# Two samples in one count matmul, evicted as 16-bit pairs, and dense layers over three tiles

## The chip, the core and the metric

The kernel runs on one NeuronCore of a Trainium2 chip. Five engines work side by side, each with its own queue in program order: TensorE (PE for its matmuls, PEld for its weight loads), VectorE (DVE), ScalarE (ACT), GpSimd (POOL) and SyncE (SP). The metric is the device time of one execution in microseconds (us): for the kernel before, the median of three runs is 7548.09 us (7520.87 to 7551.03).

## The reference

A recommender's forward pass over a batch of 16384 samples. Each sample has 32 word indices, three lists of 20 indices into small tables and four single indices:

```python
tok = word_emb[token_idx].mean(axis=1)          # 50000 x 300 table, 32 rows a sample
e1 = emb_mh1[mh1_idx].mean(axis=1)              # 1000 x 64;  e2: 5000 x 64;  e3: 10000 x 64
o1 = emb_oh1[oh1_idx]                           # 100 x 64;   o2: 50;  o3: 20;  o4: 1000
emb = jnp.concatenate([tok, e1, e2, e3, o1, o2, o3, o4], axis=1)      # 748 columns
wide = wide_mh1[mh1_idx].sum(axis=(1, 2)) + ...                       # one number a table row
h = relu(emb @ W1 + b1); h = relu(h @ W2 + b2); h = relu(h @ W3 + b3) # 1024, 512, 256
return sigmoid(h @ Wd + bd + wide)
```

## The kernel before, in words

The batch is cut into 128 tiles of 128 samples. Four streams of work run over the tiles at once.

**Words.** `tokens` issues one indirect DMA on POOL for each of the 32 word columns of a tile (line 255; 4096 in all, 128 rows of 300 floats each). Two of them fill one buffer of the pool `tok` and make a group; DVE adds a group's two halves to a running sum (lines 237, 239, 243; 16 groups a tile). The sum lags the issue by `TOK_LAG` = 3 groups in program order, and the pool has `TOK_BUFS` = 8 buffers, so a gather can be issued once the group 8 before it has been added.

**Counts.** The small tables are not gathered. Their rows are cut into 138 slices of 128 rows (`n_h`). For each sample DVE writes a one-hot of the row within the slice and a one-hot of the slice for its 64 lookups (`one_hots`, line 322). The lookups of two samples lie on the two halves of the 128 partitions. `counts` multiplies the two one-hots on TensorE, once for each half (K = 64, line 340), which gives the 128 x 138 matrix of counts of a sample; ACT evicts twelve such matrices in one instruction as fp8 (line 347). A tile has 11 steps (`STEPS`) of six pairs of samples, the last of four. There is one buffer of four PSUM banks for it (`ps_c`).

**Small sums.** `small_sums` (line 365) multiplies the counts of a whole tile (the weights: 128 samples of one slice, which lie 138 bytes apart) by the table in three bf16 terms (195 columns), 138 matmuls a tile.

**Layers.** Blocks of two tiles (`LAYER_TILES`, 256 columns, fp32) go through the three layers and the output row (lines 461, 470, 486), paced so that a block ends when the next one is ready. The last two tiles are blocks of one. A matmul in fp32 stands in the trace as two records.

The main loop is written out by hand: in each of 1424 steps it issues, in this order, the next step's one-hots, this step's count matmuls and eviction, transposes that are due, a share of the word gathers and sums, an eleventh or so of a tile's small-table matmuls and a share of the layers. Every engine keeps that order.

Of the kernel before, what the change touches and what calls it, by code (L numbers as in the profile page):

```python
# [8 lines left out]
F32 = mybir.dt.float32  # L9
# [3 lines left out]
U32 = mybir.dt.uint32  # L13
AF = mybir.ActivationFunctionType
# [10 lines left out]
TOK_BUFS = 8  # L25
# [3 lines left out]
LAYER_TILES = 2  # L29
HALF = P // 2  # L30
N_SMALL = 3 * N_MH + 4
# [20 lines left out]
def kernel(  # L52
# [42 lines left out]
    wp = ctx.enter_context(tc.tile_pool(name="wide", bufs=4))  # L95
    xsp = ctx.enter_context(tc.tile_pool(name="x_small", bufs=3))
# [3 lines left out]
    ps_c = ctx.enter_context(tc.tile_pool(name="ps_c", bufs=1, space=bass.MemoryType.PSUM))  # L100
# [47 lines left out]
    minus_half = const.tile([P, P], BF16, name="minus_half")  # L148
    nc.vector.tensor_single_scalar(minus_half, ident, -0.5, op=ALU.mult)
# [17 lines left out]
    def convert_tables():  # L167
# [19 lines left out]
        def make(p, c):  # L187

            if c == 0:
                nc.scalar.activation(term(p, 0), rows(p), AF.Copy, scale=2.0)  # L190
                return
            _, a, b = pieces[p]
            left = ps_h.tile([P, SPLIT, ROW], F32, name="left", tag="ph")[:, 0 : b - a, :]
            nc.tensor.matmul(left, ident, rows(p), start=True, stop=False)  # L194
            for k in range(c):
                nc.tensor.matmul(left, minus_half, term(p, k), start=False, stop=(k == c - 1))
            nc.scalar.activation(term(p, c), left, AF.Copy, scale=2.0)

# [67 lines left out]
    def load_indices(blk):  # L266
# [8 lines left out]
        for s in range(NSUB):  # L275
            nc.sync.dma_start(
                out=ix[(s % 2) * HALF : (s % 2 + 1) * HALF, s // 2],
                in_=idx[b0 + s * P : b0 + (s + 1) * P, IDX_MH:IDX_COLS].rearrange(
                    "(f p) c -> p f c", p=HALF
                ),  # L280
            )
# [32 lines left out]
    def one_hots(sc, s, i):  # L314
# [5 lines left out]
        for w, (one, n) in enumerate(((row1, P), (slice1, n_h))):  # L320
# [6 lines left out]
            )  # L327
        return row1, slice1

    def counts(cnt, hot, i):  # L330
# [4 lines left out]
        pc = ps_c.tile([P, 2, 2, 512], F32, name="pc")  # L335
        for k in range(rows):
            for f in range(2):
                half = slice(f * HALF, (f + 1) * HALF)
                at = k % n * n_h
                nc.tensor.matmul(  # L340
                    pc[:, f, k // n, at : at + n_h],
                    hot[0][half, k, :],
                    hot[1][half, k, :],
                    start=True,
                    stop=True,
                )
        nc.scalar.activation(  # L347
            cnt[:, :, b : b + rows, :].rearrange("l f (g k) h -> l f g (k h)", g=2),
            pc[:, :, :, 0 : n * n_h],
            AF.Copy,  # L350
            scale=0.5,
            saturate=False,
        )

    def small_sums(g, cnt):


        by_slice = cnt.rearrange("l f p h -> l (f p) h")
        for i in (0, 2, 4, 6):
            pair = SMALL[i : i + 2]  # L360
            pg = ps_g.tile([P, 2, 3 * ROW], F32, name="pg")
            for j, f in enumerate(pair):
                h0, h1 = slices[f]
                for h in range(h0, h1):
                    nc.tensor.matmul(  # L365
                        pg[:, j, :], by_slice[:, :, h], terms[:, h, :], start=(h == h0), stop=(h == h1 - 1)
# [70 lines left out]
    def early_part(block):  # L437


        part = ps_c.tile([P, 4, 512], F32, name="pc")  # L440
        for m in range(4):
            for k in range(NK - 3):
                nc.tensor.matmul(
                    part[:, m, 0 : block.n],
                    w1_sb[: chunk_k[k], k, m * P : (m + 1) * P],
                    block.chunk(k),
                    start=(k == 0),
                    stop=False,
                )
        return part  # L450

    def layer(dst, weights, bias, srcs, n_out, part=None):

        n = srcs[0].shape[-1]
        for m in range(n_out):
            begun = part is not None and m < 4
            ph = part[:, m, :] if begun else ps_h.tile([P, N], F32, name="ph", tag="ph")
# [84 lines left out]
    sizes = [LAYER_TILES] * (tiles // LAYER_TILES - 1) + [1] * LAYER_TILES  # L542
# [27 lines left out]
    for step in range(n_steps):  # L570
        t, i = divmod(step, STEPS)
        s = t % NSUB
        if i == 0:
# [7 lines left out]
            if t < tiles:  # L581
                if s == 0 and t:
                    sc = next_sc
                cnt = cp.tile([P, 2, HALF, n_h], FP8, name="cnt", tag="counts")
# [79 lines left out]
```

## Time and profile before

| | |
|---|---|
| median of three runs | 7548.09 us (7520.87 to 7551.03) |
| profiled execution: span from first to last instruction | 5191.3 us |
| busy in the span: PE, PEld | 5113.7 us (99%), 4177.5 us (80%) |
| busy in the span: DVE, ACT, POOL | 3890.9 us (75%), 2600.7 us (50%), 3888.4 us (75%) |
| mean granted TensorE clock | 0.998 |
| gathers: busy, and idle of POOL before them | 3887.5 us, 1260.5 us |

The page gives no time for the profiled execution other than its span. The median of the runs is 2356.8 us longer, and no view shows what lies in that difference. A busy PE includes matmuls that wait in its pipeline for one another, so its 99% is not a rate; the rates are read from rows of the timeline, where a burst of equal matmuls stands with its start and its count.

### The profile page before, as it was taken

Reading aid. Unit: us, or ns where it says so; the run is one execution under the profiler, and the core shown is the slowest. Engines: PE = TensorE matmul, PEld = TensorE weight load, DVE = VectorE, ACT = ScalarE, POOL = GpSimd, SP = SyncE. Lnnn points to the kernel's source line nnn. Section 1 sums busy time; section 2 is a strip of 40 time slices with the busy share of each in tenths; the row PEclk is TensorE's granted clock in tenths of the full one; section 3 lists DMA queues with packets and bytes.
Section 4 is the critical chain, followed back from the end, with each engine's and each line's share of the span. In section 5 each row is a group of like instructions: output and inputs, shape, how many; then the busy total and the mean of one; then the engine's idle time right before and its main releaser. Section 6 shows DMA issues by size and latency. Waiting matters only on the chain.

```text
span 5191.3 us, 116518 instructions
## 1 busy us (share of the span) xinstructions
PE 5113.7 (99%) x46912; PEld 4177.5 (80%) x46912; DVE 3890.9 (75%) x8502; ACT 2600.7 (50%) x2445; POOL 3888.4 (75%) x4103
## 2 busy tenths in 40 slices
PE   7999999999999999999999999999999999999999
PEld 5888888888888888888888888888888878888888
DVE  6777777777777777777777777777777777777773
ACT  6555555555545545545445455555555545555552
POOL 7777777777777777777777777777777777777774
PEclk9999999999999999999999999999999999999999
DMA  7444444444444444444444444444444444444442
GB/s 201 123 126 125 125 126 124 125 126 125 126 124 126 125 126 125 126 124 126 125 126 126 124 126 125 126 126 123 125 125 126 125 126 124 126 125 126 124 124 77
DMA packets 253019, 653.38 MB, mean 126 GB/s; under 512 B 119056, under 2 KB 119633, under 8 KB 252477
## 3 DMA queue, kind: packets, MB, share of 16 engines
q0 software_dynamic: 196608, 629.41, 44.2%
q1 hardware_dynamic: 55869, 16.53, 1.4%
q8 instruction: 367, 6.01, 0.5%
q14 instruction: 175, 1.43, 0.1%
HBM read 645.59 MB, written 0.07 MB: 124 GB/s over the span
## 4 chain that ended last, share of the span: by engine, by line
PE 94%; DVE 2%; issue 1%; DMA 1%; ACT 0%; POOL 0%; SPq 0%; DVEq 0%; ACTq 0%
PE ph L461 46%; PE pg L365 32%; PE pc L340 12%; PE po L486 1%; PE pt L426 1%; PE pt L410 1%; PE pt L407 1%; DMA tok_rows<-in_word_emb_dram,it 1%; DVE own L239 1%; DVE own L243 0%; DMA w_sb<-in_W_dram 0%; POOL tok_rows L255 0%; DVE slice L322 0%; PE left L194 0%; PE pt L427 0%
## 5 line engine op out<-in xcount | busy, mean ns | idle before, releaser
L255 POOL DMA_INDIRECT tok_rows<-in_word_emb_dram,it x4096 | 3887.5, 949 | 1260.5 <-issue 873.6
L347 ACT ACTIVATE cnt<-pc 128x1656 fp8e3<-128x1656 f32 (+1 forms) x1408 | 2124.6, 1509 | 1607.7 <-PE pc L340 1592.1
L365 PE MATMUL pg<-terms,cnt 128*128 128x195 bf16 x17664 | 1828.7, 253 | 7.9 <-DVE g L371 7.6
L365 PEld LDWEIGHTS <-cnt 128*128 128x128 fp8e3 x17664 | 1590.3, 144 | 162.1 <-issue 31.8
L461 PE MATMUL ph<-h,w_sb 128*128 128x256 f32 (+1 forms) x5200 | 1224.2, 379 | 0.5 <-ACT h L470 0.5
L461 PE MATMUL ph<-x_small,w_sb 128*128 128x256 f32 (+2 forms) x4128 | 1044.4, 381 | 4.8 <-DVE x_small L429 3.0
L461 PEld LDWEIGHTS ph<-h,w_sb 128*128 128x128 f32 x5200 | 930.8, 191 | 99.2 <-issue 0.8
L322 DVE TENSOR_TENSOR row<-own,sc 128x768 bf16<-128x768 bf16 (+1 forms) x1408 | 762.3, 541 | 304.2 <-PE pc L340 251.5
L239 DVE TENSOR_TENSOR own<-own,tok_rows 128x300 f32<-128x300 f32 x1920 | 917.0, 478 | 63.3
L243 DVE TENSOR_TENSOR own<-own,tok_rows 128x300 f32<-128x300 f32 x1792 | 856.8, 478 | 61.8
L340 PEld LDWEIGHTS <-row 64*128 64x128 bf16 x16384 | 495.4, 94 | 484.8 <-issue 227.5
L470 ACT ACTIVATE h<-ph,b_sb 128x256 f32<-128x256 f32 (+1 forms) x906 | 426.8, 471 | 912.3 <-PE ph L461 912.0
L461 PEld LDWEIGHTS ph<-x_small,w_sb 128*128 128x128 f32 (+1 forms) x4128 | 739.3, 191 | 86.6 <-PE ph L461 6.4
L322 DVE TENSOR_TENSOR slice<-own,sc 128x828 bf16<-128x828 bf16 (+1 forms) x1408 | 795.5, 565 | 0.0
L340 PE MATMUL pc<-slice,row 64*128 64x138 bf16 x16384 | 751.0, 223 | 15.8 <-DVE slice L322 9.0
L461 PE MATMUL ph<-x_tok,w_sb 128*128 128x256 f32 (+1 forms) x2064 | 565.4, 380 | 0.0
L371 DVE TENSOR_REDUCE g<-pg 128x130 f32<-128x390 f32 (+1 forms) x512 | 261.1, 510 | 393.6 <-PE pg L365 391.0
L461 PEld LDWEIGHTS ph<-x_tok,w_sb 128*128 128x128 f32 x2064 | 373.0, 192 | 40.9
L428 DVE TENSOR_SCALAR x_tok<-pt 128x256 f32<-128x256 f32 x128 | 54.4, 425 | 301.6 <-PE pt L427 301.6
L411 DVE TENSOR_TENSOR x_small<-pt,scale 128x384 f32<-128x384 f32 x128 | 71.2, 556 | 91.8 <-PE pt L410 91.8
L486 PE MATMUL po<-h,wd_sb 128*1 128x256 f32 (+1 forms) x260 | 68.0, 374 | 1.6 <-DVE x_small L429 1.0
L490 DVE TENSOR_TENSOR h<-po,wide_row 1x256 f32<-1x256 f32 (+1 forms) x65 | 26.5, 408 | 54.9 <-PE po L486 51.9
(55 smaller groups left out, 872.4 us busy)
## 6 DMA issues: line engine op xcount, KB each, us to landing
tok_rows<-in_word_emb_dram,it POOLq DMA_INDIRECT x4096
ix<-in_idx_dram SPq DMA_DIRECT2D x128, 32.0 KB
w_sb<-in_W_dram SPq DMA_DIRECT2D x6, 512.0 KB
raw<-in_mh_dram SPq DMA_DIRECT2D x4, 682.5 KB
it<-in_idx_dram SPq DMA_DIRECT2D x32, 64.0 KB
w_sb<-in_W_dram SPq DMA_DIRECT2D x1, 2048.0 KB
out_dram<-h SPq DMA_DIRECT2D x63, 1.0 KB
raw<-in_mh_dram SPq DMA_DIRECT2D x2, 227.5 KB
```

The lines of the kernel that those rows point to most:

```text
L239: nc.vector.tensor_add(tok_sum, tok_sum, a)
L243: nc.vector.tensor_add(to, tok_sum, b)
L255: nc.gpsimd.indirect_dma_start(out=rows[:, r * TOK_D : (r + 1) * TOK_D], out_offset=None, in_=word, in_offset=bass.IndirectOffsetOnAxis(ap ...
L322: nc.vector.tensor_tensor(one[:, 0:rows, :].rearrange("p i (n d) -> p i n d", d=2), iota[:, 0:n].rearrange("p (n d) -> p n d", d=2).unsque ...
L340: nc.tensor.matmul(pc[:, f, k // n, at : at + n_h], hot[0][half, k, :], hot[1][half, k, :], start=True, stop=True,)
L347: nc.scalar.activation(cnt[:, :, b : b + rows, :].rearrange("l f (g k) h -> l f g (k h)", g=2), pc[:, :, :, 0 : n * n_h], AF.Copy, scale=0 ...
L365: nc.tensor.matmul(pg[:, j, :], by_slice[:, :, h], terms[:, h, :], start=(h == h0), stop=(h == h1 - 1))
L371: nc.vector.tensor_reduce(g[:, at : at + n * ROW].rearrange("p (f d) -> p f d", f=n), pg[:, 0:n, :].rearrange("p f (c d) -> p f d c", c=3) ...
L411: nc.vector.tensor_tensor(self.small[:, 0:3, at], pt[:, 0:3, :], scale.unsqueeze(2).to_broadcast([P, 3, P]), ALU.mult)
L461: nc.tensor.matmul(ph[:, 0:n], weights[: src.shape[0], k, m * P : (m + 1) * P], src, start=(k == 0), stop=(k == len(srcs) - 1),)
L470: nc.scalar.activation(dst[:, m, 0:n], ph[:, 0:n], AF.Relu, bias=bias[:, m : m + 1])
L486: nc.tensor.matmul(po[:, 0:n], wd_sb[:, k : k + 1], h3[:, k, 0:n], start=(k == 0), stop=(k == M3 - 1))
```

## The change

The two samples of a pair now share one matmul. Their one-hots still lie on the two halves of the partitions, but the row one-hot of the upper half is multiplied by 256 (a new ACT instruction in place, on 64 partitions), and one matmul with K = 128 gives count(lower) + 256 x count(upper). ACT evicts six such matrices as 16-bit integers, whose two bytes are the two counts. Read as fp8, a byte k is the number k/64, so the table's terms are scaled by 64 where they were scaled by 2. The counts lie as slice, pair, byte: the 128 samples of one slice are contiguous. The samples of a pair are now neighbours in the batch (the index load is rearranged to match). The counts' PSUM tile halves to two banks and has two buffers.

The layers run over blocks of three tiles (384 columns), still with two blocks of one tile at the end. Six word buffers instead of eight, two buffers of small features instead of three, two of the wide rows instead of four.

```diff
-TOK_BUFS = 8
+TOK_BUFS = 6
-LAYER_TILES = 2
+LAYER_TILES = 3
+LAST_TILES = 2
+UPPER = 256.0
+COUNT = 64.0
...
-    wp = ctx.enter_context(tc.tile_pool(name="wide", bufs=4))
-    xsp = ctx.enter_context(tc.tile_pool(name="x_small", bufs=3))
+    wp = ctx.enter_context(tc.tile_pool(name="wide", bufs=2))
+    xsp = ctx.enter_context(tc.tile_pool(name="x_small", bufs=2))
...
-    ps_c = ctx.enter_context(tc.tile_pool(name="ps_c", bufs=1, space=bass.MemoryType.PSUM))
+    ps_c = ctx.enter_context(tc.tile_pool(name="ps_c", bufs=2, space=bass.MemoryType.PSUM))
...
-                nc.scalar.activation(term(p, 0), rows(p), AF.Copy, scale=2.0)
+                nc.scalar.activation(term(p, 0), rows(p), AF.Copy, scale=COUNT)
...
+        upper = row1[HALF:P, 0:rows, :]
+        nc.scalar.activation(upper, upper, AF.Copy, scale=UPPER)
         return row1, slice1
...
-        pc = ps_c.tile([P, 2, 2, 512], F32, name="pc")
+        pc = ps_c.tile([P, 2, 512], F32, name="pc")
         for k in range(rows):
-            for f in range(2):
-                half = slice(f * HALF, (f + 1) * HALF)
-                at = k % n * n_h
-                nc.tensor.matmul(
-                    pc[:, f, k // n, at : at + n_h],
-                    hot[0][half, k, :],
-                    hot[1][half, k, :],
-                    start=True,
-                    stop=True,
-                )
+            at = k % n * n_h
+            nc.tensor.matmul(
+                pc[:, k // n, at : at + n_h], hot[0][:, k, :], hot[1][:, k, :], start=True, stop=True
+            )
         nc.scalar.activation(
-            cnt[:, :, b : b + rows, :].rearrange("l f (g k) h -> l f g (k h)", g=2),
-            pc[:, :, :, 0 : n * n_h],
+            cnt[:, :, b : b + rows].rearrange("l h (g k) -> l h g k", g=2),
+            pc[:, :, 0 : n * n_h].rearrange("l g (k h) -> l h g k", h=n_h),
             AF.Copy,
-            scale=0.5,
-            saturate=False,
         )
...
-        by_slice = cnt.rearrange("l f p h -> l (f p) h")
+        by_slice = cnt.bitcast(FP8)
...
-                        pg[:, j, :], by_slice[:, :, h], terms[:, h, :], start=(h == h0), stop=(h == h1 - 1)
+                        pg[:, j, :], by_slice[:, h, :], terms[:, h, :], start=(h == h0), stop=(h == h1 - 1)
...
-    sizes = [LAYER_TILES] * (tiles // LAYER_TILES - 1) + [1] * LAYER_TILES
+    sizes = [LAYER_TILES] * ((tiles - LAST_TILES) // LAYER_TILES) + [1] * LAST_TILES
```

How it moves instructions, at two places. First ACT's queue in the middle of the program, before (`cnt<-pc` is the eviction of the counts, `h<-ph` that of a layer):

```order
L347 ACTIVATE cnt<-pc 128x2x552
L470 ACTIVATE h_31114<-ph,b_sb 128x256
L347 ACTIVATE cnt<-pc 128x2x828
L470 ACTIVATE h_31114<-ph,b_sb 128x256
L347 ACTIVATE cnt<-pc 128x2x828 x2
```

and after the change:

```order
L333 ACTIVATE row_27267<-row_27267 64x768
L347 ACTIVATE cnt<-pc 128x138x6
L471 ACTIVATE h_26592<-ph,b_sb 128x384
L333 ACTIVATE row_27307<-row_27307 64x512
L347 ACTIVATE cnt<-pc 128x138x6
```

Each step has one ACT instruction more: the scaling of the next step's row one-hot stands ahead of this step's eviction and of the layers' evictions behind it. It waits for DVE's one-hot.

Second, TensorE's queue in the last steps, in the last block of more than one tile (`ph<-h` is layer two of it; a burst of small-table matmuls stands between these rows), before:

```order
L461 MATMUL ph<-h_64807,w_sb 128x256 x9
...
L461 MATMUL ph<-h_64807,w_sb 128x256 x7
...
L461 MATMUL ph<-h_64807,w_sb 128x256 x8
...
L461 MATMUL ph<-h_64807,w_sb 128x256 x8
...
L461 MATMUL ph<-h_65061,w_sb 128x256 x7
```

and after the change:

```order
L462 MATMUL ph<-h_55354,w_sb 128x384 x9
...
L462 MATMUL ph<-h_55354,w_sb 128x384 x8
...
L462 MATMUL ph<-h_55354,w_sb 128x384 x8
...
L462 MATMUL ph<-h_55354,w_sb 128x384 x7
...
L462 MATMUL ph<-h_55589,w_sb 128x384 x8
```

The block has the same 90 matmuls in the same number of steps (11), with half as many columns again. Elsewhere a block of three tiles has 33 steps where one of two had 22.

38 lines of the change are left out of this document (21 added, 17 removed).

## The prediction

> **What bounds the kernel now.** I read the page first, for the engines' shares and the chain that ended last:
>
> ```profile
> span 5191.3 us, 116518 instructions
> PE 5113.7 (99%) x46912; PEld 4177.5 (80%) x46912; DVE 3890.9 (75%) x8502; ACT 2600.7 (50%) x2445; POOL 3888.4 (75%) x4103
> PE 94%; DVE 2%; issue 1%; DMA 1%; ACT 0%; POOL 0%; SPq 0%; DVEq 0%; ACTq 0%
> L255 POOL DMA_INDIRECT tok_rows<-in_word_emb_dram,it x4096 | 3887.5, 949 | 1260.5 <-issue 873.6
> ```
>
> By these PE is the bound and POOL has a quarter of its time free. The last row says otherwise: 3887.5 + 1260.5 = 5148.0 us is nearly the whole span. So the second view is the list of waits, for POOL:
>
> ```profile
> POOL tok_rows L255 <- issue: 873.6, 2866, 0.3
> POOL tok_rows L255 <- DVE own L239: 94.2, 309, 0.3
> POOL tok_rows L255 <- DVE own L243: 92.0, 267, 7.7
> PEld L340 <- DVE slice L322: 94.4, 256, 3.0
> ```
>
> The columns are us in total, times, longest. POOL's idle time is 0.3 us ahead of every gather, whatever is named; one wait of 7.7 us stands out. The third view is the timeline, at the start where nothing else runs, and a table of stretches in the middle:
>
> ```profile
> 5.76 0.95 POOL L255 DMA_INDIRECT tok_rows<-in_word_emb_dram,it  x1 [0.30 <-issue]
> 7.02 0.95 POOL L255 DMA_INDIRECT tok_rows<-in_word_emb_dram,it  x1 [0.30 <-issue]
> ...
> 2000.00:3000.00 1000.00, 988.98 (x9103) 808.40 (x9103) 756.19 (x1648) 500.84 (x463) 756.76 (x799) 1.00 0.46 125
> ```
>
> From start to start a gather takes 1.26 us on an idle chip, and 1000 / 799 = 1.252 us in the middle (the last count of the row is POOL's). The gathers run at their own pace and never wait: 4096 x 1.252 = 5128 us, from 3.1 us on. A step has 4096 / 1424 = 2.88 of them, 3.60 us. Now TensorE's step:
>
> ```profile
> 2503.03 0.54 PE L340 MATMUL pc<-slice,row 64*128 64x138 bf16 x12
> ...
> 2503.50 1.43 PE L365 MATMUL pg<-terms,cnt 128*128 128x195 bf16 x14
> ...
> 2504.77 1.92 PE L461 MATMUL ph<-h,w_sb 128*128 128x256 f32 x8
> ...
> 2506.62 0.55 PE L340 MATMUL pc<-slice,row 64*128 64x138 bf16 x12
> ```
>
> From counts to counts 3.59 us: 0.47 for the counts, 1.27 for the small sums, 1.85 for the layers, by their starts. So TensorE and POOL are level, within 0.01 us a step. Whatever makes TensorE's step shorter than 3.60 us leaves POOL's 5128 us standing. That is the core of this prediction.
>
> **The change part by part.** Rows for matmuls of other sizes:
>
> ```profile
> 1680.30 0.40 PE L305 MATMUL pk<-ident_bf,keys 128*128 128x128 bf16 x4 [1.14 <-DVE wide_row L415]
> ...
> 1680.53 1.21 PE L365 MATMUL pg<-terms,cnt 128*128 128x195 bf16 x12
> ```
>
> ```profile
> 159.12 2.62 PE ph L461 x12
> ...
> 5148.02 6.95 PE ph L461 x62
> ```
>
> The *counts*. Four full-height bf16 matmuls of 128 columns, each with its own weight load, take 0.23 us to the start of the next burst: 0.0575 each. Ten columns more add 0.23/4 x 10/128 = 0.0045, so a matmul of 138 columns takes 0.062 us, and six take 0.37 us where twelve half-height ones took 0.47: 0.10 us less a step. The twelve ran two at a time, so halving their number saves no streaming; the saving is what the burst lost on leaving the half-height form. The *small sums* now load weights that lie contiguous: 1.27 / 14 = 0.091 us each before, against 0.0575 + 67 x 0.00045 = 0.088 by the row of 128 columns; bounds 0 and 0.04 us a step, I take 0.03. The *layers*: a record of 256 columns takes 2.62 / 12 = 0.2183 us, one of 128 columns (the last block's) 6.95 / 62 = 0.1121; on that line 384 columns take 0.3245, 1% less per column: 0.017 us of the 1.75 us a step. Sum 0.15 us a step, 1408 steps with counts: 211 us of TensorE work, bounds 0.12 and 0.16 us. TensorE's step becomes 3.44 us. It is hidden whole behind POOL's 3.60 us; the cover would be gone only if POOL weren't the pace.
>
> The Trainium skill, TensorEngine Tiling (Array Packing), section Key Properties, says that a change of tiling mode drains the engine. The rows agree at the end of the count burst, as above. By that rule its beginning is freed as well: eight layer records took 1.85 us where 8 x 0.2183 = 1.75, so another 0.10 us a step, 141 us, of TensorE work. I don't count it, as a switch from fp32 to bf16 stays there; hidden behind POOL it changes nothing.
>
> *ACT*. Rows by form:
>
> ```profile
> L347 ACT ACTIVATE cnt<-pc 128x1656 fp8e3<-128x1656 f32 x1280 | 1985.4, 1551 | 1512.6 <-PE pc L340 1497.0 <-issue 11.8 <-PE pg L365 2.4
> L470 ACT ACTIVATE h<-ph,b_sb 128x256 f32<-128x256 f32 x882 | 418.0, 474 | 880.7 <-PE ph L461 880.4
> L347 ACT ACTIVATE cnt<-pc 128x1104 fp8e3<-128x1104 f32 x128 | 139.3, 1088 | 95.1 <-PE pc L340 95.1
> L190 ACT ACTIVATE terms<-raw 128x455 bf16<-128x455 f32 x19 | 11.0, 577 | 0.0
> ```
>
> (1551 - 1088) / 552 = 0.839 ns an element and 162 ns fixed. The new eviction, 828 elements: 0.86 us, if its order of elements costs nothing; at worst as long as the old one, 1.55. The scaling of the upper half, 768 elements: 0.162 + 0.644 = 0.81 us, and by the row L190, which reads SBUF as it does (577 against 544 by the line), 0.84; below, half of that if two-byte elements go two at a time. A step had 1.51 + 0.30 us of ACT work (2124.6 and 426.8 us over 1408) and now has 0.86 + 0.84 + 0.25 = 1.95, at worst 2.64. It fits into 3.60. Behind the scaling stand this step's eviction and the layers' evictions, and TensorE's layer output after the next waits for the latter. The counts' second PSUM buffer takes the eviction off TensorE's path. I take 0.
>
> *Two buffers of small features, two of wide rows*: a block's features are last read in its first layer (48 of 90 matmuls, so by step 18 of its 33), its wide row at step 33; the next block but one fills the same buffers from step 34 on. 0.
>
> *Six word buffers*. A gather must now find the group 6 before it added. At the start, while the tables are converted, the sums are late:
>
> ```profile
> 83.37 0.95 POOL L255 DMA_INDIRECT tok_rows<-in_word_emb_dram,it  x1 [0.30 <-DVE own L243]
> ...
> 88.84 0.48 DVE L243 TENSOR_TENSOR own<-own,tok_rows 128x300 f32<-128x300 f32 x1
> ...
> 89.58 0.94 POOL L255 DMA_INDIRECT tok_rows<-in_word_emb_dram,it  x1 [1.51 <-DVE own L243]
> ```
>
> By count, the first row is the 65th gather and opens group 33; the DVE row ends group 27 at 89.32. With six buffers that gather waits 5.95 us, the most of this stretch, and POOL never makes it up. I take +5 us, bounds 0 (each step's counts leave earlier) and 12 (ACT's new instruction among the table's). In the middle:
>
> ```profile
> 5069.04 0.94 POOL L255 DMA_INDIRECT tok_rows<-in_word_emb_dram,it  x1 [0.30 <-issue]
> ...
> 5079.51 0.48 DVE L239 TENSOR_TENSOR own<-own,tok_rows 128x300 f32<-128x300 f32 x1
> ```
>
> These are the last gather of group 2020 and its first addition, 9.5 us after the gather's end. Six buffers leave 5 x 2.5 = 12.5 us, less 1 us for the two additions: 2 us of room here. Had TensorE kept its 3.59 us step, it would now and then be used up. With 3.44 the sums come sooner; I take no stall, and 3 us off because the last blocks begin that much earlier (bounds 0 and 7).
>
> *The end*. The last block of three tiles starts where the last of two did and has the same 11 steps. TensorE is the bound there:
>
> ```profile
> 5080.00:5132.00 52.00, 51.70 (x349) 44.91 (x347) 19.98 (x45) 12.18 (x18) 34.12 (x36) 1.00 0.40 111
> 5132.00:5191.00 59.00, 52.24 (x418) 49.07 (x418) 17.40 (x42) 11.82 (x32) 11.37 (x12) 0.91 0.12 32
> ...
> 5134.82 0.95 POOL L255 DMA_INDIRECT tok_rows<-in_word_emb_dram,it  x1 [7.75 <-DVE own L243]
> ```
>
> PE is busy 51.70 of 52 us and POOL is stalled by late sums (the 7.75 us). 90 matmuls of two records cost 180 x (0.3245 - 0.2183) = +19.1 us, less 1 us for the saved switches: +18 us. It is work that in the middle would have been hidden. POOL's last gathers, which start two groups (5 us) later by the smaller pool, have their 12 us between 5149.5 and the last addition.
>
> Sum: +5 - 3 + 18 = +20 us on the span, 5211. The median of the runs stands 2357 us above the span, and no view shows why. If that is a constant, the time is 7548 + 20 = 7568; if everything is slower by 7548 / 5191 = 1.454, it is 7577. I take **7568 us**.
>
> **The rivals.** *TensorE sets the pace in the runs* (0.27, faster). The 2357 us could be a slower TensorE or a quicker POOL outside the profile. For it: PE carries 94% of the chain. Against: the granted clock was 1.00 in the row of stretches, and the gather's 1.25 us doesn't depend on its neighbours. Then 211 - 18 = 193 us come off: 7355; with everything times 1.454, 7267. With the skill's second drain, 7214.
>
> *ACT's scaling gets into the chain* (0.16, slower). Before, 256 steps' counts waited for DVE's slice (the row in the waits), which ends 0.58 us after the row one-hot. The scaling ends 0.84 us after it, and later where ACT is in an eviction of 0.86 (or 1.55) us: 0.26 to 1.8 us more for each, 67 to 460 us. It decides from 0.16 us a step, 225 us, on, where TensorE's step passes POOL's: up to 235 us on top, about 7680 in the middle of that. Against it: the one-hots are made a step ahead.
>
> *Six buffers stall POOL all through* (0.05, slower). If the sums' lag passes 11.5 us in the middle, each such cluster costs POOL some us for good; 25 clusters of 3 us: 7643.
>
> *The change does not do what it says* for TensorE (its burst keeps the loss): then its step stays 3.57 and the forecast's time stands; it is in the forecast's share.
>
> **How the numbers follow.** Forecast 0.52, own range 7540 to 7595. A measurement of this kernel tells 0.5% (38 us, 7510 to 7586) from no change. Of the forecast's share 0.49 lies within and 0.03 above, and the slower rivals add 0.21: faster 0.27, same 0.49, slower 0.24. The range takes in the milder form of the first rival and most of the slower ones: 7350 to 7660. Outside I leave 0.12 below and 0.08 above.
>
> **What would show it.** Right: gathers at 1.25 us from start to start with no wait in the middle; a row `pc` x6 with about 0.37 us to the next burst; PE's busy share lower, with idle time ahead of the counts; layer bursts of about 5 us a step in the last block and a longer wait of POOL there; a span of 5200 to 5220. Wrong: a span below 5150, which needs a quicker gather; waits of the counts' weight loads for ACT; waits of POOL for L247 in the middle; or a time that moves while the span doesn't, which would place the cause in the 2357 us.

## The result and the profile after

The changed kernel takes **7104.03 us** (median of 4 runs, 7065.27 to 7113.1) where the kernel before takes 7548.26 us (7520.87 to 7551.03): a ratio of **0.9407** (95% interval 0.9379 to 0.9435), faster by 444 us. Forecast were 7568 us and no change. This time the profiled execution is one of the timed ones: its span is 7111.3 us, its time 7113.1.

The chip matters. The experiments below ran on six chips, each set of runs on one of them: on two the kernel before takes 7544 and 7577 us, on four about 5194. The profile of before (5191.3 us) is of the second kind, the timed runs of this section are of the first; which chips those were is not on record. Below, a chip is called disturbed or undisturbed by that. One execution of the changed kernel on an undisturbed chip (12252.1 us at a granted clock of 0.403, where nine others took 5189 to 5193 us) is left out of the ratios.

The page of the changed kernel: its first lines, the granted clock by slices, the gathers, and the weight loads of the small sums:

```profile
span 7111.3 us, 94821 instructions
PE 5573.0 (78%) x34940; PEld 3857.5 (54%) x34940; DVE 3874.2 (54%) x8481; ACT 2756.1 (39%) x3538; POOL 3877.1 (55%) x4103
PEclk8888888888888888898888988888888888888889
L259 POOL DMA_INDIRECT tok_rows<-in_word_emb_dram,it x4096 | 3876.2, 946 | 3194.5 <-DVE own L247 1892.0
L363 PEld LDWEIGHTS <-cnt 128*128 128x128 fp8e3 x17664 | 1659.7, 105 | 1031.4 <-issue 982.9
```

No engine is busy for as much as 80%. POOL, which was said never to wait, is idle for 3194.5 us (its 0.3 us ahead of every gather included). TensorE's weight loads are idle for 982.9 us in one group with nothing to wait for that the profile shows ("issue"). The list of waits says it from both sides (us in total, times, longest):

```profile
POOL tok_rows L259 <- DVE own L247: 1892.0, 536, 18.9
PEld L363 <- issue: 982.9, 913, 7.1
DVE row L326 <- remote: 867.4, 162, 9.5
ACT h L471 <- remote: 809.7, 134, 12.2
```

("remote" is a release that the trace doesn't name. Where it was followed up, it is TensorE: an eviction of the counts that waited 6.87 us for "remote" begins at 2499.23 us, 0.06 us after the start of the last count matmul.) One such place in the timeline, first POOL, then TensorE's matmuls, then its weight loads:

```profile
2482.14 0.94 POOL L259 DMA_INDIRECT tok_rows<-in_word_emb_dram,it  x1 [6.05 <-DVE own L247]
...
2489.64 0.94 POOL L259 DMA_INDIRECT tok_rows<-in_word_emb_dram,it  x1 [0.30 <-issue]
2490.89 0.95 POOL L259 DMA_INDIRECT tok_rows<-in_word_emb_dram,it  x1 [0.30 <-issue]
2493.04 0.94 POOL L259 DMA_INDIRECT tok_rows<-in_word_emb_dram,it  x1 [1.21 <-DVE own L247]
```

```profile
2487.05 0.53 PE L344 MATMUL pc<-slice,row 128*128 128x138 bf16 x6
2487.42 1.45 PE L363 MATMUL pg<-terms,cnt 128*128 128x195 bf16 x15
2488.71 1.48 PE L462 MATMUL ph<-h,w_sb 128*128 128x384 f32 x4
2490.03 0.53 PE L344 MATMUL pc<-slice,row 128*128 128x138 bf16 x6
2490.40 0.85 PE L363 MATMUL pg<-terms,cnt 128*128 128x195 bf16 x8
2492.03 0.33 PE L363 MATMUL pg<-terms,cnt 128*128 128x195 bf16 x2 [0.78 <-issue]
2493.46 0.41 PE L363 MATMUL pg<-terms,cnt 128*128 128x195 bf16 x3 [1.10 <-issue]
2494.91 0.33 PE L363 MATMUL pg<-terms,cnt 128*128 128x195 bf16 x2 [1.03 <-issue]
```

```profile
2491.33 0.10 PEld L363 LDWEIGHTS <-cnt 128*128 128x128 fp8e3 x1 [0.31 <-issue]
...
2492.06 0.10 PEld L363 LDWEIGHTS <-cnt 128*128 128x128 fp8e3 x1 [0.64 <-issue]
...
2492.75 0.10 PEld L363 LDWEIGHTS <-cnt 128*128 128x128 fp8e3 x1 [0.60 <-issue]
...
2493.48 0.16 PEld L363 LDWEIGHTS <-cnt 128*128 128x128 fp8e3 x2 [0.63 <-issue]
...
2494.18 0.10 PEld L363 LDWEIGHTS <-cnt 128*128 128x128 fp8e3 x1 [0.54 <-issue]
```

Until 2491 a step goes as it should. Then TensorE gets one or two pairs of weight load and matmul every 0.7 us, and the trace shows nothing that they wait for. Below, this is called a dribbling stretch. POOL had issued eight gathers in a row since its wait of 6.05 us. The delay then comes back to POOL: TensorE is late, DVE's one-hots are late behind it, so are the sums that stand behind those in DVE's order, and POOL stalls. A row of the table of stretches shows that the clock isn't the cause at this place (after the length come the busy times and counts of PE, PEld, DVE, ACT and POOL, the granted clock, the share of the DMA engines and GB/s):

```profile
2491.00:2500.00 9.00, 4.84 (x31) 2.88 (x30) 3.37 (x8) 2.11 (x3) 4.62 (x5) 1.00 0.38 102
```

PE is busy 4.84 of 9 us at a granted clock of 1.00. Count as a dribbling stretch every place where at least four weight loads, with no more than 2.5 us from one to the next, start over 0.45 us after the load before them: there are 253, of 9.6 us on average, 2434 us in all. The same count finds 38, 355 us, in the changed kernel's trace from an undisturbed chip, where TensorE waits or runs at the halved clock. Over the disturbed execution the clock is halved in 273 periods, 1743 us in all. They begin 4.9 us (median) after the last stretch has begun, so by their order they are a consequence of the stretches and not their cause. What they cost is worked out in experiment 3.

### The profile page after: what moved, and what is told of

It is laid out like the page before. It is cut to its first block, busy times and chain, and to the rows that moved or that the text cites. A ratio compares the mean times of both kernels' runs of the same rounds, so it can differ in the third digit from the quotient of the medians.

```text
span 7111.3 us, 94821 instructions
## 1 busy us (share of the span) xinstructions
PE 5573.0 (78%) x34940; PEld 3857.5 (54%) x34940; DVE 3874.2 (54%) x8481; ACT 2756.1 (39%) x3538; POOL 3877.1 (55%) x4103
## 4 chain that ended last, share of the span: by engine, by line
PE 48%; another core or an unknown queue 18%; DVE 15%; issue 13%; ACT 3%; POOL 1%; DMA 1%; DVEq 0%; SPq 0%; POOLq 0%; ACTq 0%
PE ph L462 23%; PE pg L363 16%; PE pc L344 6%; DVE own L247 4%; DVE own L243 4%; DVE slice L326 3%; DVE row L326 2%; ACT row L333 1%; ACT cnt L347 1%; POOL tok_rows L259 1%; DVE g L369 1%; ACT h L471 1%; PE po L487 1%; PE pt L408 1%
## 5 line engine op out<-in xcount | busy, mean ns | idle before, releaser
L259 POOL DMA_INDIRECT tok_rows<-in_word_emb_dram,it x4096 | 3876.2, 946 | 3194.5 <-DVE own L247 1892.0
L363 PE MATMUL pg<-terms,cnt 128*128 128x195 bf16 x17664 | 2078.6, 265 | 881.8 <-issue 563.7
L363 PEld LDWEIGHTS <-cnt 128*128 128x128 fp8e3 x17664 | 1659.7, 105 | 1031.4 <-issue 982.9
L347 ACT ACTIVATE cnt<-pc 128x828 uint16<-128x828 f32 (+1 forms) x1408 | 1190.0, 845 | 1798.8 <-remote 919.9
L333 ACT ACTIVATE row<-row 64x768 bf16<-64x768 bf16 (+1 forms) x1408 | 1155.2, 820 | 937.9 <-DVE row L326 772.3
L462 PE MATMUL ph<-h,w_sb 128*128 128x384 f32 (+1 forms) x3520 | 1374.5, 530 | 39.1 <-issue 34.0
L462 PE MATMUL ph<-x_small,w_sb 128*128 128x384 f32 (+1 forms) x2784 | 1152.0, 538 | 60.8 <-issue 48.9
L344 PEld LDWEIGHTS <-row 128*128 128x128 bf16 x8192 | 638.0, 103 | 912.4 <-issue 491.5
L344 PE MATMUL pc<-slice,row 128*128 128x138 bf16 x8192 | 812.6, 233 | 283.1 <-ACT row L333 150.5
L471 ACT ACTIVATE h<-ph,b_sb 128x384 f32<-128x384 f32 (+1 forms) x612 | 349.7, 572 | 1497.0 <-remote 809.7
L462 PEld LDWEIGHTS ph<-x_small,w_sb 128*128 128x128 f32 x2784 | 540.7, 213 | 381.1 <-issue 183.8
L462 PE MATMUL ph<-x_tok,w_sb 128*128 128x384 f32 (+1 forms) x1392 | 568.2, 513 | 15.8 <-issue 15.8
```

What stands on the lines that cost most here:

```text
L259: nc.gpsimd.indirect_dma_start(out=rows[:, r * TOK_D : (r + 1) * TOK_D], out_offset=None, in_=word, in_offset=bass.IndirectOffsetOnAxis(ap ...
L333: nc.scalar.activation(upper, upper, AF.Copy, scale=UPPER)
L344: nc.tensor.matmul(pc[:, k // n, at : at + n_h], hot[0][:, k, :], hot[1][:, k, :], start=True, stop=True)
L347: nc.scalar.activation(cnt[:, :, b : b + rows].rearrange("l h (g k) -> l h g k", g=2), pc[:, :, 0 : n * n_h].rearrange("l g (k h) -> l h g ...
L363: nc.tensor.matmul(pg[:, j, :], by_slice[:, h, :], terms[:, h, :], start=(h == h0), stop=(h == h1 - 1))
L462: nc.tensor.matmul(ph[:, 0:n], weights[: src.shape[0], k, m * P : (m + 1) * P], src, start=(k == 0), stop=(k == len(srcs) - 1),)
```

## The experiments

On record two theories stood at first. **S**: the extra time goes with TensorE's instructions, which the page's queue q8 fetches in blocks of 16 KiB (367 before, 276 after; 2357/367 = 6.4 us and (7104 - 5191)/276 = 6.9 us a block). **W**: the changed kernel is only quicker by TensorE's work, the profile of 5191 us stands for the kernel before, and without stretches the gathers set the pace as predicted.

**1. The kernel before, and the change in parts, all gathers.** The runs fell on an undisturbed chip. The kernel before, unchanged:

> The kernel before, unchanged, profiled again. Theory S (TensorE's instructions arrive late: in the changed kernel's trace TensorE gets its instructions only every 0.7 us for about 9 us at a time, some 250 times, about once per 16 KiB of its instruction stream, and the clock falls to half behind each): span about 7545 us, clock near 0.87, and such stretches about once for each of the 367 fetches of 16 KiB. Theory W (the changed kernel is only quicker by TensorE's work, and the 5191 us profile stands for the kernel before): span about 5190 us without such stretches.

5193.21 us, span 5191.1: the profile of before was no accident, and the time is the span + 2 us. The 2357 us above it belong to the chip, not to every run.

The counts part alone (here and below some edits are shortened to the values that change):

```diff
 # the changed kernel, with
-TOK_BUFS = 6;  LAYER_TILES = 3;  wide bufs=2;  x_small bufs=2
+TOK_BUFS = 8;  LAYER_TILES = 2;  wide bufs=4;  x_small bufs=3
```

> Only the counts part of the change (stacked pairs, 16-bit eviction, scaling, two PSUM buffers); blocks of two tiles and the old numbers of buffers. 64 fetches of 16 KiB fewer than before, 29.5 more than the whole change. S, with the slope of the whole change (444 us / 91 fetches = 4.9 us a fetch): 7548 - 64 x 4.9 = 7235 us, ratio 0.958. W (TensorE's work, 0.15 us a step nearly all in the counts): 7120 us, ratio 0.943.

5167.63 us, ratio 0.9949 (0.9933 to 0.9966). The layers part alone:

```diff
 # the kernel before, with
-TOK_BUFS = 8;  LAYER_TILES = 2;  wide bufs=4;  x_small bufs=3
+TOK_BUFS = 6;  LAYER_TILES = 3;  LAST_TILES = 2;  wide bufs=2;  x_small bufs=2
```

> Only the layers part (blocks of three tiles, six word buffers, two and two of the others); the counts as before. 29.5 fetches fewer. S: 7548 - 29.5 x 4.9 = 7404 us, ratio 0.981. W: TensorE's layer work falls by 1%, 7530 us, ratio 0.997; if the six buffers cost something, above 7548.

5208.24 us, ratio 1.0026 (1.0016 to 1.0036). Its list of waits:

```profile
POOL tok_rows L256 <- DVE own L244: 152.6, 375, 16.7
DVE x_tok L429 <- PE pt L428: 253.5, 119, 25.1
```

The longest waits, 16.7 and 25.1 us, lie at 5159 and 5155 us, in the end that the prediction priced at +18. And the changed kernel with layers over single tiles:

```diff
-LAYER_TILES = 3
+LAYER_TILES = 1
```

> The changed kernel with blocks of one tile (128 columns): the same columns through the layers, but 15120 more weight-load and matmul pairs, 118 more fetches of 16 KiB. S: 7104 + 118 x 4.9 = 7680 us, slower than the kernel before. W: 22784 records of 0.1121 us for 7696 of 0.3235, +64 us of work: 7170 to 7200 us.

5163.97 us, ratio 0.9942 (0.9922 to 0.9962): 118 more blocks of instructions than in the changed kernel cost nothing here. The expectations of the last three runs were all worked out from 7548 us; on this chip they could not be tested, and S could neither hold nor fall.

**2. The change itself, and TensorE alone.** On another undisturbed chip:

> The changed kernel itself, beside the kernel before. Theory W (without the dribbling stretches the gathers set the pace, as the prediction worked it out; the counts part gave -26 us and the layers part +14 us when run alone): about 5180 us where the kernel before takes 5194, ratio 0.997 (0.993 to 1.001), POOL's gathers 1.252 us from start to start, under 10 halved-clock periods. Where the kernel before takes about 7550 us, theory S (the extra time goes with the number of TensorE's instructions, 276 blocks of 16 KiB against 367) expects about 7100 us again. A third possibility, that the change itself brought its 6% and the two chips only differ in level, expects 0.94 x 5194 = 4884 us.

5191.66 us where the kernel before takes 5194.18: ratio **0.9996** (0.9986 to 1.0006). There the forecast of no change holds. To see TensorE without POOL, both kernels with 2 of every 32 gathers of a tile; the group's rows are added 16 times, so DVE's work stays and the token part of the output is another:

```diff
-                rows = tokp.tile([P, TOK_GROUP * TOK_D], F32, name="tok_rows")
-                for r in range(TOK_GROUP):
+                if q == 0:
+                    rows = tokp.tile([P, TOK_GROUP * TOK_D], F32, name="tok_rows")
+                for r in range(TOK_GROUP if q == 0 else 0):
```

> The kernel before with 2 of every 32 gathers of a tile (the rows of the first group are added 16 times; the token part of the output is therefore another): POOL's pace is gone, everything else stands. If TensorE is level with POOL, as the prediction has it (3.59 us against 3.60 us a step), the time falls by no more than 80 us: 5110 to 5190 us where the kernel before takes 5194. If the gathers were the sole bound with TensorE well below, it falls to under 5000. If it runs where the kernel before takes 7550: unchanged within 2% if TensorE's instruction supply sets the pace there, lower by more than 500 us if the gathers' DMA traffic is what holds the supply up.

> The changed kernel with the same 2 of 32 gathers. It shows what the change is worth to TensorE alone. By the prediction's own sum (0.15 us a step of 1408 and +18 us at the end) it is 190 us below the kernel before with few gathers, about 4940; with both ends of the count burst freed (0.25 us a step) 330 us below, about 4800 us. If ACT's scaling sat in the chain it would be no lower than that kernel. On a chip where the kernel before takes 7550: about 6900 to 7100 us.

5193.9 us, the same as with all gathers, and 4844.85 us (0.9327 of the kernel before, 0.9309 to 0.9346), between the 4940 and 4800 us that were expected. So without the gathers' pace the kernel before is no quicker: TensorE by itself takes its whole time. The change takes **349 us** off that. PE in the timeline, before and after, both with few gathers:

```profile
2502.98 0.54 PE L341 MATMUL pc<-slice,row 64*128 64x138 bf16 x12
2503.45 1.43 PE L366 MATMUL pg<-terms,cnt 128*128 128x195 bf16 x14
2504.72 1.92 PE L462 MATMUL ph<-h,w_sb 128*128 128x256 f32 x8
2506.57 0.55 PE L341 MATMUL pc<-slice,row 64*128 64x138 bf16 x12
```

```profile
2502.95 0.54 PE L345 MATMUL pc<-slice,row 128*128 128x138 bf16 x6
2503.32 1.46 PE L364 MATMUL pg<-terms,cnt 128*128 128x195 bf16 x15
2504.62 2.12 PE L463 MATMUL ph<-x_small,w_sb 128*128 128x384 f32 x6
2506.58 0.53 PE L345 MATMUL pc<-slice,row 128*128 128x138 bf16 x6
```

The counts take 0.37 us to the next burst, as forecast (0.47 before). The layers' burst takes 1.96 us to the counts: 6 records at the forecast's 0.3245 are 1.95, so nothing is lost there, where before eight records took 1.85 against 1.75. The new form frees both ends of the count burst. (The Trainium skill, TensorEngine Tiling (Array Packing), Key Properties, has a change of tiling mode drain the engine; the rows bear that out at both ends, about 0.10 us each.) Last, single-tile layers with all gathers and eight buffers:

```diff
-TOK_BUFS = 6;  LAYER_TILES = 3
+TOK_BUFS = 8;  LAYER_TILES = 1
```

> The changed kernel with layers over single tiles (128 columns, 394 instead of 276 blocks of 16 KiB of TensorE's instructions) and eight word buffers. Theory W: within 3 us of the 5164 us that the same kernel with six buffers took, because the gathers set the pace; theory S, where the kernel before takes 7550: 276 to 394 blocks at 4.9 to 6.5 us, 7680 to 7870 us, slower than before; if instead the work of TensorE were what is slowed, about 7100 + 0.017 us x 2 a step = 7150 us.

5158.44 us, ratio 0.9931 (0.9915 to 0.9948), the fastest with all gathers on an undisturbed chip, and 5.5 us under the 5164 of six buffers (within 3 was expected).

**3. The parts with few gathers: a disturbed chip.** The same cut of gathers in the counts part, the layers part and the single-tile layers. This time the kernel before took 7543.77 us beside them (7517.99 to 7571.72).

> The counts part alone (layers still over two tiles, eight word buffers), with 2 of every 32 gathers of a tile, so that TensorE is alone; the token part of the output is therefore another. Of the 349 us that the whole change takes off TensorE's own time, the prediction's terms give 0.10 us a step for the counts and 0.03 for the small sums, 183 us; the second freed end of the burst 141 us more, 324 us. Theory D (both ends of the half-height burst drained TensorE): 4850 to 4870 us. Theory L (the larger layer blocks carry what the prediction's terms do not give): about 5010 us. Should the kernel before take 7550 us here, theory T (TensorE's own time is stretched by one factor, 7548/5191 = 1.454 and 7104/4843 = 1.467) expects 1.46 x 4860 = 7100, theory S (time per 16 KiB of its instructions, 306 blocks) 4860 + 306 x 6.6 = 6880.

> The layers part alone (blocks of three tiles, six word buffers), with 2 of 32 gathers. Theory D: the layers save 0.017 us a step (24 us) and lose 18 us in the last block: 5185 us, within 10. Theory L: about 5040 us. Should the kernel before take 7550 us here: theory T 1.46 x 5185 = 7570, theory S 5185 + 337 x 6.6 = 7410.

> The changed kernel with layers over single tiles and 2 of 32 gathers: 50,060 instead of 34,940 pairs of weight load and matmul, for nearly the same streaming. By the rows of 128 and 256 columns (0.1121 against 0.2183/2) a step's layers cost 0.046 us more than over two tiles, 65 us, and the end is some 20 us shorter than with two: about 4900 us, 60 above the changed kernel's 4845. If the number of instructions cost TensorE time by itself here (theory S without any disturbance), it is above 5100. Should the kernel before take 7550 us here: theory T 1.46 x 4900 = 7150, theory S 4900 + 394 x 6.6 = 7500.

4849.04, 5200.28 and 4932.81 us, with a granted clock of 0.996 to 0.999: with 2 of 32 gathers **the disturbance is gone**. Both readings on record for this case fall, S (6880, 7410, 7500) and T, a factor of 1.46 on TensorE's own time (7100, 7570, 7150). What holds TensorE up goes with the gathers. The times themselves are near those expected of an undisturbed TensorE (4850 to 4870, 5175 to 5195 and about 4900 us; they miss by 1, 5 and 33 us). So they still split the 349 us: the counts part takes 5194 - 4849 = 345 us off, the layers part adds 6; 10 us of the 349 stay unassigned. The counts part also shows the second end of the count burst with the layers as before: eight records of 256 columns ahead of the counts take 1.752 us (median) where they took 1.849.

The changed kernel's page on the disturbed chip, beside its page with few gathers, splits the loss: PE is busy 5573.0 us in place of 4743.7, 829 us more, and idle 1538.3 us in place of 98.9. The first is close to half of the 1743 us at the halved clock (872 us, an estimate that takes all of that time as busy), the second is TensorE held up. So over a third of the loss comes by way of the clock, though the clock only follows.

**4. What of the gathers?** Four kernels, which fell on an undisturbed chip, and so tell nothing of the disturbance:

> The changed kernel with 16 of every 32 gathers of a tile (each gathered group is added twice; the token part of the output is another). With 2 of 32 it took 4845 us. Where the kernel before takes 7550 us: theory G (each gather costs TensorE a fixed time: (7104 - 4843)/3840 = 0.59 us) expects 4845 + 0.59 x 1792 = 5900 us; a threshold (the supply is only disturbed above some load) expects 4845 to 4900; an all-or-nothing disturbance expects about 7100. Where the kernel before takes 5194: 4845 us.

> The changed kernel with all 4096 gathers, each of 128 rows, but of 16 bytes a row instead of 1200 (the token part of the output is another; VectorE adds as many elements as before). Where the kernel before takes 7550 us: if the number of gathers (their instructions, descriptors and packets) disturbs TensorE, about 7100 us; if the bytes moved do (theory B), about 5190, set by POOL's 1.25 us a gather. Where the kernel before takes 5194: about 5190.

> The changed kernel with layers over single tiles and eight word buffers (394 instead of 276 blocks of 16 KiB of TensorE's instructions), all gathers. Its TensorE alone took 4933 us. Where the kernel before takes 7550 us: theory G expects 4933 + 2261 = 7190 us; theory S (the loss goes with TensorE's instructions) 4933 + 2261 x 394/276 = 8160; theory T (a factor of 1.46 on TensorE's own time while gathers run) 7200. Where the kernel before takes 5194: 5158.

> The changed kernel with each gather replaced by a plain load of 128 neighbouring rows of the same table, issued by SP: the same 629 MB in rows of 1200 bytes into the same buffers, but no POOL instruction and no descriptors made by POOL (the token part of the output is another). Where the kernel before takes 7550 us: about 7100 if the traffic disturbs TensorE, 4845 to 4950 if the descriptors that POOL makes do. Where the kernel before takes 5194: 4845 to 4950, TensorE being alone at its own pace.

4846.75 us with half the gathers, 5191.21 with rows of 16 bytes, 5159.86 for the single tiles, 4848.81 with plain loads. They do show what POOL's pace is made of: it doesn't change with the bytes (5191.21 against 5191.66 us, 946 ns busy a gather in both) and is gone when SP loads the same 629 MB as neighbouring rows. To have all the cases in one execution, the next kernels change them by stretches of tiles (the edit of the third, shortened; the first two have `kind = t // STRETCH`, four stretches of 32 tiles: all gathers, all with 16 bytes a row, plain loads, half of them):

```diff
+                kind = KINDS[t // STRETCH]
...
+                    if kind == 2:
+                        at = (t * N_TOK + j) % 64 * P
+                        nc.sync.dma_start(out=rows[...], in_=word[at : at + P, :])
+                        continue
+                    size = TINY if kind == 1 else TOK_D          # TINY = 4 floats
...                  # kind 3: 16 of 32 gathers, kind 4: 2 of 32
```

> The changed kernel, whose 128 tiles get their word rows in four ways, 32 tiles each: all 32 gathers as they are; all 32 gathers of 16 bytes a row; plain loads of neighbouring rows by SP, 1200 bytes a row; 16 of 32 gathers (the token part of the output is another). Where the kernel before takes 5194 us: POOL's pace in the first two stretches (32 x 32 x 1.252 = 1282 us each), TensorE's own in the last two (4845/4 = 1211 us each), about 5000 us in all. Where the kernel before takes 7550 us: the first stretch takes 7104/4 = 1776 us; the second takes the same if the number of gathers disturbs TensorE, 1282 if their bytes do; the third 1776 if the traffic does, 1211 if only the descriptors made by POOL do; the fourth 1211 + 32 x 14 x 0.59 = 1475 us with a cost per gather, 1211 with a threshold. TensorE's granted clock by stretch (0.88 disturbed, 0.98 to 1.00 not) shows the same.

> The kernel before, whose 128 tiles get their word rows in four ways, 32 tiles each: all 32 gathers as they are; all 32 gathers of 16 bytes a row; plain loads of neighbouring rows by SP, 1200 bytes a row; 16 of 32 gathers (the token part of the output is another). Where the kernel before takes 5194 us: 5191/4 = 1298 us in each stretch, since TensorE alone takes as long as with all gathers, about 5195 in all. Where the kernel before takes 7550 us: the first stretch takes 7548/4 = 1887 us; the second takes the same if the number of gathers disturbs TensorE, 1298 if their bytes do; the third 1887 if the traffic does, 1298 if only the descriptors made by POOL do; the fourth 1298 + 32 x 14 x 0.61 = 1571 us with a cost per gather, 1298 with a threshold.

Both ran on undisturbed chips. The changed kernel takes 5013.74 us, with stretches of 1264, 1274, 1178 and 1181 us (from the first count eviction of a stretch to that of the next). The kernel before takes 5194.29 us, with four stretches of 1269 to 1276. Both are what was expected for such chips, within 33 us a stretch, and tell nothing of the disturbance. The third:

> The changed kernel, whose 128 tiles get their word rows in eight stretches of 16 tiles: all gathers, all gathers of 16 bytes a row, all, plain loads by SP, all, 16 of 32 gathers, 2 of 32, all (the token part of the output is another). Where the kernel before takes 5194 us: 16 x 32 x 1.252 = 641 us with all gathers or small ones, 606 us with plain loads, half and few. Where the kernel before takes 7550 us: 888 us with all gathers, 606 with 2 of 32; small ones 888 if the number of gathers disturbs TensorE and 641 if their bytes do; plain loads 888 if the traffic does and 606 if only the descriptors made by POOL do; half of the gathers 606 + 16 x 14 x 0.59 = 738 with a cost per gather, 606 with a threshold.

It fell on a disturbed chip (the kernel before beside it: 7577.01 us) and took 6241.55 us, in a single execution. The table of its eight stretches, with the columns as above:

```profile
0.00:884.00 884.00, 648.86 (x4093) 455.74 (x4093) 479.66 (x1065) 362.75 (x476) 489.14 (x523) 0.86 0.38 102
884.00:1764.00 880.00, 691.88 (x4310) 476.01 (x4309) 482.50 (x1053) 339.75 (x433) 476.36 (x505) 0.87 0.06 3
1764.00:2628.00 864.00, 693.15 (x4349) 480.16 (x4346) 482.05 (x1053) 339.39 (x432) 482.08 (x510) 0.88 0.34 91
2628.00:3230.00 602.00, 587.38 (x4304) 435.65 (x4305) 482.24 (x1053) 339.94 (x432) 5.88 (x7) 0.99 0.47 131
3230.00:4061.00 831.00, 674.57 (x4305) 467.37 (x4303) 481.41 (x1048) 339.83 (x433) 465.51 (x492) 0.90 0.36 96
4061.00:4668.00 607.00, 586.37 (x4321) 435.02 (x4319) 484.48 (x1056) 339.63 (x432) 255.73 (x271) 0.99 0.27 71
4668.00:5253.00 585.00, 579.56 (x4312) 431.82 (x4310) 480.99 (x1052) 338.83 (x431) 44.00 (x46) 1.00 0.06 14
5253.00:6121.00 868.00, 699.02 (x4336) 479.12 (x4334) 476.79 (x1037) 339.34 (x433) 444.80 (x470) 0.88 0.32 85
```

In order: all gathers 884 us; all with 16 bytes a row **880**; all 864; plain loads **602**; all 831; half of them **607**; 2 of 32 585; all 868. The bytes don't matter: 3 GB/s disturb as much as 102. The traffic doesn't: 131 GB/s by plain loads leave the clock at 0.99. What is left are POOL's gathers themselves: their instructions, the descriptors that they make, or the scattered rows that they read, where the plain loads read neighbouring ones; these three were not separated. And it is no price per gather: 225 more gathers cost 22 us (607 - 585), the next 239 some 257 (864 - 607).

How the gathers lie in time fits that. In the half stretch they come in pairs, and the next pair starts 3.2 us (median) after the second gather of the last one, where in a row it is 1.25. For the changed kernel's own trace on its disturbed chip, from 100 to 7000 us, this is where in an unbroken row of gathers (starts under 1.5 us apart) POOL stood when a dribbling stretch of TensorE began:

```
gather of the row         1    2    3    4    5    6    7    8    9   10   11+
gathers at that place   522  511  428  428  385  385  322  322  206  204  291
stretches begun there    11    8    1    4   10   40  103   36   19   12    5
```

Of 249 stretches 179 begin at the 6th to 8th gather; the middle half of all begin 7.4 to 9.1 us after POOL resumed. The half stretch has only two, each at the 7th gather of the only two long rows in it, which have 12 each. Whether the row's length decides or the rate over some microseconds was not separated. What a gather does to TensorE's instructions isn't shown by any view: the fetches of TensorE's 16 KiB blocks (276 in the changed kernel) take 0.98 us (median) on the disturbed chip and 1.02 on the undisturbed one, and start at the same places of the program. Why two of six chips show it stays open too. (The Trainium skill, DMA: Bandwidth & Descriptors, Latency and other measured facts, guesses at contention on the ports of the rings in SBUF that hold software-made descriptors, as the reason why two of the DMA engines are usually slower, and says that descriptors made by hardware have no such ring. It doesn't speak of TensorE. The plain loads, which the profile lists as hardware_dynamic and which take 602 us, fit a cause on that path; no run here shows a ring or a port.)

## Why the prediction was wrong

**The step that failed** is the last of the sum: the median stands 2357 us above the span, "If that is a constant, the time is 7548 + 20". It isn't one: for the changed kernel it is 7104 - 5192 = 1912 us. In the timed runs TensorE and POOL were not level: TensorE was held up while the gathers ran, TensorE set the pace, and POOL waited 1892.0 us for late sums. There TensorE's saving isn't hidden. Of the 444 us, 349 are TensorE's own (5193.9 to 4844.85 with few gathers); the loss above that went from 7548 - 5194 = 2354 to 7104 - 4845 = 2259 us, 95 less. That the loss moves so little fits a disturbance by gathers, which are the same 4096; why it moves by 95 is open. How the 444 us split between counts, layers and buffers on a disturbed chip wasn't measured: the parts ran there with few gathers only. No trace of the kernel before on a disturbed chip was kept; its granted clock there, 0.876 to 0.879, is that of the changed kernel (0.875 to 0.880). The last sign of being wrong that the prediction named has come: the time moved by 444 us and the span on an undisturbed chip by 3.

It was the rival *TensorE sets the pace in the runs*, held at 0.27 with 7355 us, or 7214 with the second drain. What spoke against it ("the granted clock was 1.00", "the gather's 1.25 us doesn't depend on its neighbours") was read in an execution that had none of the 2357 us in it, and so could say nothing of them. With a third of the measured time unexplained, that span was no ground for 0.52.

The other steps, in their order:

- **POOL and TensorE level at 3.60 us a step.** The rows were right (1.252 us a gather, 3.59 us a step), the choice between them wrong by a little: without 30 of 32 gathers the kernel before takes 5193.9 against 5194.2 us, so TensorE's own pace gives its whole time, and POOL was at most just covered. Before (experiment 1), the last gather starts at 5148.5 us; with the counts part alone at 5128.4.
- **TensorE's 211 us.** Too small: 349. The count burst is right (0.37 us). The uncounted 0.10 us at the other end is there, 141 us; the reason for leaving it out, that a switch from fp32 to bf16 stays, didn't hold, since the layers' burst loses nothing now with that switch still behind it. Counts and small sums gave 345 us in place of 183 + 141 = 324. The small sums are under-sized too, and their reason doesn't fit: with few gathers a burst of 15 takes 1.293 us where it took 1.355, and a burst of one 0.083 where it took 0.143 (medians). That is some 0.06 us a burst whatever its length, where 0.03 us a step was taken for weights that lie contiguous; further matmuls of a burst are no quicker (0.087 us each before, 0.086 after). What the fixed part is stays open. The layers part adds 6 us to TensorE's own time, where 18 - 24 = -6 was the forecast.
- **ACT.** Scaling 0.81 to 0.84 us, eviction 0.86: the page has

```profile
L333 ACT ACTIVATE row<-row 64x768 bf16<-64x768 bf16 (+1 forms) x1408 | 1155.2, 820 | 937.9 <-DVE row L326 772.3
L347 ACT ACTIVATE cnt<-pc 128x828 uint16<-128x828 f32 (+1 forms) x1408 | 1190.0, 845 | 1798.8 <-remote 919.9
```

  Each makes 1% of the chain of that page; with few gathers all of ACT makes 1%, and the kernel runs at TensorE's pace. The waits of the counts' weight loads for the scaling, which the prediction named as a sign, are there: 127.4 us (145 times) on an undisturbed chip, 249.7 us (152 times) on the disturbed one, 36.6 us with few gathers. They did not make the kernel slower on either kind of chip, so the rival with ACT's scaling falls. The rival *Six buffers stall POOL* looks right by the 1892.0 us, but on undisturbed chips POOL has no such waits; whether eight buffers would shorten the loss on a disturbed chip wasn't tried, since the kernels with eight buffers and all gathers fell on undisturbed ones.
- **Six buffers, the end.** On the undisturbed chip POOL waits 4.7 us beyond its usual 0.3 in the first 200 us (0.7 before, the first gather left out) and 24.1 us in the last 120 (6.8 before): +4 where +5 was forecast, and +17 where the forecast put +18 on TensorE. Its longest wait there:

```profile
POOL tok_rows L259 <- DVE own L247: 275.8, 811, 16.8
```

- **The sum on the span**, +20, came out as -3 (5188.1 against 5191.1): the terms that cost came out near their size, and the term for earlier sums, -3, was too small: the counts part alone gave -26. Its gathers are busy 3875.5 us in place of 3890.6 and idle 1252.3 in place of 1257.4, so the last one starts 20 us earlier; why a gather is shorter (946 ns for 950) isn't shown. In the whole change the last gather starts 6 us later than before (5154.7 us), and what follows it is 9 us shorter. That the sum is off by only 23 us owes something to terms of both signs.

## What to carry to other kernels

A measured time that the profiled span doesn't reach is not a constant to be carried along: it is the larger part of the question, and what the profile says of who sets the pace holds only for the span. Two engines within 1% of each other are one bound, and a change to one of them is worth its full size wherever the other turns out not to set the pace. An experiment that takes one of them away (2 of 32 gathers) tells at once what the other needs by itself. A kernel that depends on back-to-back gathers by POOL deserves timing on more than one chip.

## What was not expected of the hardware

On two of six chips, TensorE's instructions are held up while POOL issues gathers back to back: some 7 in a row, then about 9.6 us in which one or two pairs of weight load and matmul come every 0.7 us. In the one execution that compares the cases, it is independent of the bytes (880 us at 3 GB/s, 884 at 102) and absent with plain loads (602 at 131 GB/s) and nearly so with gathers in spaced pairs (607). The kernel before takes 7544 us on such a chip and 5194 on the others. DVE, ACT and the gathers themselves (0.946 us busy, as elsewhere) keep their durations.
